# The last 3x3 convolution in tiles of four columns, with new pacing of the work beside the samplings

## Chip, cores, metric

The kernel runs on one core of a Trainium2 chip. The metric is the device time of one execution in microseconds; the profile of one execution is read along with it.

## What is computed

Four blocks act on `x` of 4 images x 256 channels x 64 x 64, each on a group norm of `x` and added back to it. The fourth adds its own input, too.

```python
x = x + _L0_conv_ref(_gn(x), ...)   # 1x1 conv, depthwise 3x3, deformable sampling, outproj, squeeze, two linear maps
x = x + _L1_conv_ref(_gn(x), ...)   # qkv 1x1, depthwise 5x5, linear attention, proj
x = x + _L2_conv_ref(_gn(x), ...)   # 3x3 convolution, 256 -> 256, weights scale*sign(w)
x = x + _L3_conv_ref(_gn(x), ...)   # attention against 2x2-pooled keys, 1x1 conv
```

In block 0 each pixel, group (4) and point (9) gathers four neighbours at computed places. Block 2 is an ordinary 3x3 convolution:

```python
scale = jax.lax.stop_gradient(jnp.mean(jnp.abs(real_w), axis=(1, 2, 3), keepdims=True))
bin_no_grad = scale * jnp.sign(real_w)
...
return jax.lax.conv_general_dilated(x, bin_w, window_strides=(STRIDE, STRIDE), padding=[(PAD, PAD), (PAD, PAD)], ...)
```

## The kernel before

All data is float32. Channels lie on the 128 partitions in two halves (`KT`), pixels on the free axis.

The images go through in a pipeline. For each image `sample` runs 288 rounds. A round issues four indirect DMAs on POOL (L596), which fetch table rows into one of seven buffers `g`, and eight small matmuls (L603) that weigh and sum them into `acc`, one bank in two halves. Two rounds fill a half; then ACT copies it (L608), PE turns it (L613), ACT copies again (L623). Every 18 rounds `project` (L636) applies the output projection. ACT makes the weights `wm` (L588).

`beside` (in `run`) interleaves other generators into these rounds. Each has a total of costs and a span `lo` to `hi` of the rounds' share. After each round a generator is advanced while what it has spent, by the numbers that it yields, is behind its due part of the total. What is left at `hi` is emitted at once. Beside the sampling of image n run:

- `feedforward` (end of block 0) of image n-1, from 0 to 0.22, total `FEED`
- `layer1` (block 1) of image n-1, from 0.22 to 1, total `LINEAR`
- `second`: `layer2` and then `layer3` (blocks 2 and 3) of image n-2, from 0.22 to 1, total `SECOND`; only beside the samplings of images 2 and 3
- `binarise`, the convolution's weights, beside the sampling of image 1, from 0 to 0.2

Inside `ordered()` PE, DVE, ACT and POOL run their instructions in the order in which they are emitted. An instruction that waits holds up everything behind it on its engine. Outside it the framework's scheduler sets the order.

`layer1` keeps a list `later` of closures, of which `step` pops one at each yield; a closure adds a `cost` of its own (L803). `summed` (L898) closes the sums of one half of the attention, `output` (L913) computes one band of its result, with `head` (L931) taking a bank for each `rden`. `groupnorm` (L112) needs two small matmuls with DVE work between.

After the last sampling come the last `feedforward` and `layer1` beside most of `second` for image 2, then the last `layer2` beside the rest of `second`, outside `ordered()`, and at the end the last `layer3`.

`layer2` convolves pairs of columns from four transformed inputs (two outputs from four products instead of six). It works on bands of 8 rows: `normed` loads and scales ten rows, `parts` (L1039) makes four sums and differences, 48 matmuls of 256 columns follow (L1088), and `leave` (L1068 to L1072) combines the products and adds the input.

```python
                        ps = self.long().rearrange("p (e q) -> p e q", e=2)
                        for i in range(12):
                            e, k, t = i // 6, i // 3 % 2, i % 3
                            nc.tensor.matmul(ps[:, e], w[:, k, t, 2 * half + e, m * P:(m + 1) * P], v[:, 2 * half + e, k, t:t + 8],
                                             start=i % 6 == 0, stop=i % 6 == 5)
```

`long` takes banks `acc` and `dp` in turn once the samplings are over. `layer3` computes scores (L1188), their maximum and exponential, turns them (L1200), multiplies by the values (L1206), scales (L1211), and after four such steps applies a 1x1 convolution (L1216) and adds the scaled input `r` (L1217, L1218).

Of the kernel before, what the change touches and what calls it, by code (L numbers as in the profile page):

```python
# [17 lines left out]
P = 128  # L18
# [18 lines left out]

CONVOLVE, OFFSETS, BINARY = NB * 9 + 26, 60, 62  # L40
FEED = NB * 40 + 8
LINEAR, LAST = 956, 624
STEPS, BEGUN = 900, 0.22
CONV, SECOND = NB * 22.5 + 11, 568
EPS_BN = 1e-5
EPS_GN = 1e-5
EPS_ATT = 1e-5
# [24 lines left out]
class Net:  # L72
# [36 lines left out]
        for k in range(KT):  # L109
            self.nc.vector.bn_stats(st[:, k, b, :], x[:, k])  # L110

    def groupnorm(self, pool, st, name):  # L112

        nc = self.nc
        mv = pool.tile([P, KT, 2], F32, name=name + "_mv")
        for k in range(KT):
            nc.vector.bn_aggr(mv[:, k, :], st[:, k].rearrange("p b s -> p (b s)"))
        yield 2
        pg = self.ps(name + "_pg")
        nc.tensor.matmul(pg[:, 0:KT], self.bd8, mv[:, :, 0], start=True, stop=True)  # L120
        mg = pool.tile([P, KT], F32, name=name + "_mg")
        nc.vector.tensor_copy(mg, pg[:, 0:KT])
        d = pool.tile([P, KT], F32, name=name + "_d")
        nc.vector.tensor_tensor(d, mv[:, :, 0], mg, ALU.subtract)
        nc.vector.tensor_tensor(d, d, d, ALU.mult)
        nc.vector.tensor_tensor(d, d, mv[:, :, 1], ALU.add)
        yield 2
        pv = self.ps(name + "_pv")
        nc.tensor.matmul(pv[:, 0:KT], self.bd8, d, start=True, stop=True)
        sc = self.rsqrt(pool, pv[:, 0:KT], EPS_GN, KT, name)  # L130
        bi = pool.tile([P, KT], F32, name=name + "_bi")
        nc.vector.scalar_tensor_tensor(bi, mg, -1.0, sc, ALU.mult, ALU.mult)
        yield 4
        return sc, bi

    def folded(self, pool, out, w, sc, bi, name):
# [67 lines left out]
    def setup(self):  # L204
# [45 lines left out]

        self.s_d = [dt([HW * PT, G * 5], F32, name=f"sd{n}") for n in im]
        self.w2_d = dt([P, KT, 3, 4, C], F32, name="w2")

    def binarise(self):


        nc = self.nc
        parts = [(k, slice(t, t + 3)) for k in range(KT) for t in range(0, 9, 3)]
        with self.tc.tile_pool(name="bin", bufs=1, side="left") as sp, \
                self.tc.tile_pool(name="bin2", bufs=2, side="left") as bp:  # L260

            def real(part):
                k, t = part
                w = bp.tile([P, 3, C], F32, name="w")
                nc.sync.dma_start(w, self.a["w2T"][:, k, t])
                return w

            sums = sp.tile([P, 6, C], F32, name="sums")
            for i, part in enumerate(parts):
                w = real(part)  # L270
                yield 1
                t = bp.tile([P, 3, C], F32, name="t")
                nc.vector.scalar_tensor_tensor(t, w, -1.0, w, ALU.mult, ALU.max)
                nc.vector.tensor_reduce(sums[:, i], t.rearrange("p t o -> p o t"), AX.X, ALU.add)
                yield 2
            ps = self.ps()
            for i in range(6):
                nc.tensor.matmul(ps[:, 0:C], self.ones, sums[:, i], start=i == 0, stop=i == 5)
            scale = sp.tile([P, C], F32, name="scale")
            nc.scalar.activation(scale, ps[:, 0:C], AF.Copy, scale=1.0 / (C * 9))  # L280
            yield 2
            for part in parts:
                w = real(part)
                yield 1
                t = bp.tile([P, 3, C], F32, name="t")
                s = bp.tile([P, 3, C], F32, name="s")
                nc.vector.tensor_scalar(t, w, 0.0, None, ALU.is_lt)
                nc.vector.scalar_tensor_tensor(s, w, 0.0, t, ALU.is_gt, ALU.subtract)
                nc.vector.tensor_tensor(s, s, scale.unsqueeze(1).to_broadcast([P, 3, C]), ALU.mult)
                yield 3  # L290
                nc.vector.tensor_scalar(t, w, -1.0, 1.0, ALU.max, ALU.min)
                nc.vector.tensor_tensor(s, s, t, ALU.subtract)
                nc.vector.tensor_tensor(s, s, t, ALU.add)
                yield 2
                u = bp.tile([P, 4, C], F32, name="u")
                nc.scalar.copy(u[:, 0], s[:, 0])
                nc.scalar.activation(u[:, 1], s[:, 2], AF.Copy, scale=-1.0)
                nc.scalar.activation(t[:, 0], s[:, 1], AF.Copy, scale=0.5)
                nc.vector.tensor_tensor(t[:, 1], s[:, 0], s[:, 2], ALU.add)
                for e, op in ((2, ALU.add), (3, ALU.subtract)):  # L300
                    nc.vector.scalar_tensor_tensor(u[:, e], t[:, 1], 0.5, t[:, 0], ALU.mult, op)
                nc.sync.dma_start(self.w2_d[:, part[0], part[1].start // 3], u)
                yield 2


# [451 lines left out]
    def layer1(self, n, st, st2):  # L757
# [3 lines left out]
        with tc.tile_pool(name=f"la{n}", bufs=1, side="right") as sp, \  # L761
# [35 lines left out]
            def staged(items):  # L797


                for i in range(len(items) + max(map(len, items)) - 1):  # L800
                    now = [it[i - k] for k, it in enumerate(items) if 0 <= i - k < len(it)]
                    later.append(lambda now=now: [f() for f in now])
                    later[-1].cost = 1.1  # L803

            sums = self.ps1.tile([P, 2, 2, P], F32, name="vk", tag="vk")
            ks = [sp.tile([P, 2, NB], F32, name=f"ks{t}") for t in range(2)]
# [91 lines left out]
            def summed(t):  # L898

                ln = bp.tile([P, 2, P], F32, name="ln", tag="v1")  # L900
                pc = self.ps("comb").rearrange("p (e o) -> p e o", e=2)
                for kind in range(2):
                    j = 2 * kind + t
                    nc.vector.tensor_tensor(ln[:, kind], sums[:, t, kind], self.con("bd"), ALU.mult)
# [1 line left out]
                    nc.vector.tensor_reduce(kk, ks[t][:, kind, 0:(NB, NCH)[kind]], AX.X, ALU.add)  # L906
                    for h in range(2):
                        nc.vector.tensor_scalar(ld[:, j, h, 16 * h:16 * h + 16], self.con("oh"), kk, None, ALU.mult)
                for kind in range(2):
                    nc.tensor.matmul(pc[:, kind], ln[:, kind], pw[:, 2 * kind + t], start=True, stop=True)  # L910
                    nc.vector.tensor_copy(pw[:, 2 * kind + t], pc[:, kind])

            def output(c, qp, aq):  # L913
# [17 lines left out]
                def head(h, j):  # L931
                    if not j:
                        xv.append(self.block(bp, self.x3_d[n], 2 * c + h, "xq", bufs=room(1)))
                    hs, i = slice(64 * (j // 2), 64 * (j // 2) + 64), 2 * h + j % 2
                    vk = alone and next(spare) == "vk"
                    pb[h, j] = self.ps1.tile([P, 512], F32, name="rden", tag="vk") if vk else self.ps("rden")
                    nc.tensor.matmul(pb[h, j], self.con("sel")[hs, i * P:(i + 1) * P], rd[0][hs], start=True, stop=True)  # L937

# [85 lines left out]
                    yield from aggregate(*args, **more)  # L1024
                    number += 1
            while later:
                yield step(2 if alone else 1)


    def layer2(self, n, st, st3, side="left"):  # L1030
# [3 lines left out]
        with tc.tile_pool(name=f"ca{n}", bufs=1, side=side) as sp, \  # L1034
                tc.tile_pool(name=f"cb{n}", bufs=2, side=side) as bp:
            w = sp.tile([P, KT, 3, 4, C], F32, name="w2")
            nc.sync.dma_start(w, self.w2_d)
            sc, bi = yield from self.groupnorm(sp, st, "g2")
            add = lambda out, a, b, op=ALU.add: (nc.gpsimd if self.alone else nc.vector).tensor_tensor(out, a, b, op)  # L1039

            def normed(b):
# [58 lines left out]
            before.pop()()  # L1100


    def layer3(self, n, st, wide=False):
        nc, tc, a = self.nc, self.tc, self.a
        M = HW // 4
        with tc.tile_pool(name=f"na{n}", bufs=1, side="left") as sp, \
# [6 lines left out]
            nc.sync.dma_start(gw, a["g_wT"])  # L1113
            ww = sp.tile([P, C], F32, name="ww")
            nc.sync.dma_start(ww, a["wz_wT"])
            sc, bi = yield from self.groupnorm(sp, st, "g3")

            sc1 = sp.tile([P, KT], F32, name="sc1")
            nc.vector.tensor_scalar(sc1, sc, 1.0, None, ALU.add)
# [1 line left out]
            nc.vector.tensor_tensor(bi1, bi, self.vec("wz_b", n=2), ALU.add)  # L1121

            bb = sp.tile([P, KT, P], F32, name="bb")
            ps = self.ps()
            for k in range(KT):
                nc.vector.tensor_scalar(bb[:, k], self.ones, bi[:, k:k + 1], None, ALU.mult)
                nc.tensor.matmul(ps[:, 0:P], bb[:, k], gw[:, k], start=k == 0, stop=k == KT - 1)
            gb = sp.tile([P, P], F32, name="gb")
            nc.vector.tensor_tensor(gb, ps[:, 0:P], self.row("g_b"), ALU.add)
# [46 lines left out]
            for b in range(NB):  # L1176
                m2 = bp.tile([P, 512], F32, name="m2")
                for j in range(4):
# [25 lines left out]
                    ps = self.ps()  # L1204
                    for m in range(8):
                        nc.tensor.matmul(ps[:, 0:P + 1], pT[:, m], gt[:, m], start=m == 0, stop=m == 7)  # L1206
                    yield 1.5
                    rden = bp.tile([P, 1], F32, name="rden")
                    nc.vector.reciprocal(rden, ps[:, P:P + 1])
                    yield 1.5  # L1210
                    nc.scalar.activation(m2[:, j * P:(j + 1) * P], ps[:, 0:P], AF.Copy, scale=rden)  # L1211
                yield 1.5
                r = self.block(bp, self.x5_d[n], b, "r5", bufs=1)
                for k in range(KT):
                    ps = self.ps()
                    nc.tensor.matmul(ps, ww[:, k * P:(k + 1) * P], m2, start=True, stop=True)  # L1216
                    nc.scalar.activation(r[:, k], r[:, k], AF.Identity, bias=bi1[:, k:k + 1], scale=sc1[:, k:k + 1])  # L1217
                    nc.vector.tensor_tensor(r[:, k], r[:, k], ps, ALU.add)  # L1218
                nc.sync.dma_start(self.out[n, :, b * 512:(b + 1) * 512].rearrange("(k p) s -> p k s", p=P), r)

    def run(self):
# [40 lines left out]
        with self.tc.tile_pool(name="gather", bufs=2, side="left") as self.gp, \  # L1262
# [16 lines left out]
            with ordered():  # L1279
                beside(self.sample(1, ssum[1]), rounds, (self.binarise(), BINARY, 0, 0.2), *behind(0))  # L1280
                for n in range(2, N):
                    beside(self.sample(n, ssum[n]), rounds, *behind(n - 1), (second(n - 2), SECOND, BEGUN, 1))
        self.idle, self.alone, self.spare = cycle(["acc", "dp"]), True, True
        rest = second(N - 2)
        with ordered():
            beside(range(STEPS), STEPS, (feed(N - 1), FEED, 0, 0.27), (linear(N - 1), LAST, 0.27, 1), (rest, SECOND, 0.27, 1.05))
        self.spare = False
        beside(range(STEPS), STEPS, (conv(N - 1, "right"), CONV, 0, 1), (rest, 150, 0, 1))

        self.banks = cycle(["mm", "mm", "mm", "vk"])  # L1290
        for _ in pooled(N - 1, True):
# [95 lines left out]
```

## Time and profile before

| | us |
|---|---|
| median of 3 runs (7638.07 to 7640.4) | 7640.25 |
| time of the profiled execution | 7631.35 |
| its span | 7629.6 |
| first gather, last gather (L596) | 138.8, 6117.3 |
| last `feedforward` (L714 to the last L749) | about 6180 to 6402 |
| last `layer1`, beside `second` of image 2 | about 6402 to 7232 |
| last `layer2` | about 7232 to 7418 |
| last `layer3` | about 7418 to 7630 |

Busy over the span: PE 5886.1 us (77%), POOL 4936.3 (65%), DVE 4810.4 (63%), ACT 3530.1 (46%). A row of the trace for PE is half of a float32 matmul of the program: the last convolution's 384 matmuls are 768 rows. The matmul rows overlap, so their mean duration is more than the distance from one to the next. A wait is put down to the instruction that ended last.

### The profile page before, as it was taken

To read this page: it belongs to the slowest core of one execution; us is meant where nothing else is said; L and a number is where in the kernel's file an instruction comes from. 1 tells how busy PE (TensorE), PEld (TensorE's weight loads), DVE (VectorE), ACT (ScalarE), POOL (GpSimd) and SP (SyncE) were. 2 spreads that over 40 slices of the span, in tenths; PEclk is the share of its full clock that TensorE was granted. 3 is DMA by queue.
4 is the path that set the end of the run, shared out by engine and by line. 5 is a ranking of instruction groups with operands and counts; after the bars stand their busy time and mean duration, and the time that the engine had idled before them with its cause. 6 is when DMAs were issued, how large, how long until landed. Compare 5 with 4: busy or idle time off the path is not lost. (4 is left out here: it accounts for less than half of the span.)

```text
span 7629.6 us, 99735 instructions
## 1 busy us (share of the span) xinstructions
PE 5886.1 (77%) x35776; PEld 3454.3 (45%) x35776; DVE 4810.4 (63%) x6045; ACT 3530.1 (46%) x10767; POOL 4936.3 (65%) x4870
## 2 busy tenths in 40 slices
PE   5676666678766677888877778988677789967899
PEld 2333333334433333346644443466444445744487
DVE  6454543633688776228988872279888734999623
ACT  2443433444545443445555544454555523655415
POOL 2777777777777777777777676777776702866210
PEclk7676776779877777999988889999888899988999
DMA  6564655565544444555544445455544432210221
GB/s 185 150 188 140 174 170 145 168 185 164 167 124 131 125 141 135 171 150 154 158 147 138 134 138 175 135 168 156 153 133 140 130 103 71 72 53 34 73 81 51
DMA packets 744383, 1031.75 MB, mean 135 GB/s; under 512 B 354128, under 2 KB 459984, under 8 KB 742352
## 3 DMA queue, kind: packets, MB, share of 16 engines
q0 software_dynamic: 221184, 604.27, 27.4%
q1 hardware_dynamic: 522704, 421.10, 18.6%
q8 instruction: 283, 4.64, 0.3%
q14 instruction: 212, 1.74, 0.1%
HBM read 856.39 MB, written 168.61 MB: 134 GB/s over the span
## 5 line engine op out<-in xcount | busy, mean ns | idle before, releaser
L596 POOL DMA_INDIRECT g<-tab,sl x4608 | 4401.1, 955 | 1715.8 <-issue 1271.0
L178 DVE SCALAR_TENSOR_TENSOR agg<-pad,vec,agg 128x1024 f32<-128x1024 f32 x2280 | 2933.7, 1287 | 64.4
L603 PE MATMUL acc<-g,wm 128*32 128x128 f32 x18432 | 1264.0, 321 | 1161.9 <-ACT at L608 670.8
L588 ACT ACTIVATE wm<-sl,con 128x48 f32<-128x48 f32 x6144 | 1487.8, 365 | 23.6 <-DMA sl<-sd 11.9
L603 PEld LDWEIGHTS acc<-g,wm 128*32 128x32 f32 x18432 | 622.1, 121 | 1836.7 <-ACT at L608 888.3
L1088 PE MATMUL ps<-xd,w 128*128 128x256 f32 x3072 | 721.6, 386 | 8.0 <-DVE x L1072 3.5
L1088 PEld LDWEIGHTS ps<-xd,w 128*128 128x128 f32 x3072 | 579.9, 194 | 116.6 <-issue 35.6
L623 ACT COPY dT<-dp 64x128 f32<-64x128 f32 x1152 | 295.5, 256 | 646.4 <-PE dp L613 379.7
L739 PE MATMUL ps<-x2f,f 128*128 128x512 f32 x1024 | 489.8, 625 | 4.0 <-ACT f L714 4.0
L724 DVE SCALAR_TENSOR_TENSOR hm<-ps,vec,lk 128x512 f32<-128x512 f32 x256 | 191.9, 750 | 466.7 <-ACT lk L741 466.2
L824 PE MATMUL ps<-xr,qw 128*128 128x512 f32 x768 | 461.1, 732 | 13.8 <-ACT pT L1202 5.2
L749 PE MATMUL ps<-hm,f 128*128 128x512 f32 x1024 | 468.0, 604 | 0.0
L1039 POOL TENSOR_TENSOR xd<-xp 128x640 f32<-128x640 f32 x64 | 79.6, 1270 | 514.2 <-ACT xp L1051 416.1
L608 ACT COPY at<-acc 128x256 f32<-128x256 f32 x576 | 214.1, 372 | 423.1 <-PE acc L603 411.2
L741 ACT ACTIVATE lk<-ps,low 128x512 f32<-128x512 f32 x256 | 175.9, 687 | 500.5 <-PE ps L739 498.2
L1206 PEld LDWEIGHTS ps<-gt,pT 128*128 128x128 f32 x2048 | 282.6, 216 | 85.9 <-ACT pT L1202 43.4
L1206 PE MATMUL ps<-gt,pT 128*128 128x129 f32 x2048 | 297.6, 304 | 29.8 <-ACT pT L1202 29.1
L613 PE MATMUL dp<-ident,at 128*128 128x128 f32 x1152 | 265.2, 317 | 65.7 <-ACT dT L623 62.9
L636 PE MATMUL po<-dT,ow 128*128 128x288 f32 x1024 | 297.3, 438 | 21.8 <-ACT dT L631 8.9
L1188 PE MATMUL s<-ph,th 128*128 128x512 f32 x512 | 281.6, 663 | 32.9 <-DVE ot L941 11.0
L200 POOL TENSOR_TENSOR ak<-ak,m 128x1024 f32<-128x1024 f32 x96 | 227.6, 2371 | 117.2 <-ACT m L196 112.8
L727 DVE TENSOR_TENSOR xyf<-xyf,ps 128x512 f32<-128x512 f32 x64 | 44.0, 687 | 402.1 <-PE ps L749 389.3
(243 smaller groups left out, 7565.2 us busy)
## 6 DMA issues: line engine op xcount, KB each, us to landing
g<-tab,sl POOLq DMA_INDIRECT x4608
x<-x SPq DMA_DIRECT2D x128, 512.0 KB
xr<-x SPq DMA_DIRECT2D x96, 512.0 KB
tab<-xo SPq DMA_DIRECT2D x192, 128.0 KB
x<-in_x SPq DMA_DIRECT2D x32, 512.0 KB
y<-yc SPq DMA_DIRECT2D x32, 512.0 KB
yb<-y SPq DMA_DIRECT2D x64, 256.0 KB
x<-yb SPq DMA_DIRECT2D x64, 256.0 KB
```

The costliest lines, as they stand in the source:

```text
L178: nc.vector.scalar_tensor_tensor(to, s, wt, acc, ALU.mult, ALU.add)
L588: nc.scalar.activation(wm[:, :, :, o], blocks[b][:, r:r + WR, G:], AF.Copy, scale=self.con("own")[:, o:o + 1])
L596: nc.gpsimd.indirect_dma_start(out=g[:, i, :], out_offset=None, in_=table, in_offset=bass.IndirectOffsetOnAxis(ap=sl.bitcast(I32)[:, r, i: ...
L603: nc.tensor.matmul(acc[32 * i:32 * i + 32, :], wm[:, r4, 4 * i + 2 * x:4 * i + 2 * x + 2, :], g[:, i, x * P:(x + 1) * P], start=x == 0, st ...
L623: nc.scalar.copy(dT[b][hs, :, r:r + UR], dp[u][hs, :, :, s, :].rearrange("p v g o -> p g v o"))
L636: nc.tensor.matmul(po[m][:, 0:BR * OB], self.ow[:, k, m * P:(m + 1) * P], dT[b][:, k].rearrange("p r o -> p (r o)"), start=k == 0, stop=k ...
L739: nc.tensor.matmul(ps, f1[:, k, m * P:(m + 1) * P], x2[:, k], start=k == 0, stop=k == KT - 1)
L749: nc.tensor.matmul(ps, f2[:, k, m * P:(m + 1) * P], hm[:, k], start=k == 0, stop=k == 4 * KT - 1)
L824: nc.tensor.matmul(ps, qw[:, k, m * P:(m + 1) * P], x[:, k], start=k == 0, stop=k == KT - 1)
L1088: nc.tensor.matmul(ps[:, e], w[:, k, t, 2 * half + e, m * P:(m + 1) * P], v[:, 2 * half + e, k, t:t + 8], start=i % 6 == 0, stop=i % 6 == 5)
L1188: nc.tensor.matmul(s[i], tv[:, 4 * b + j], ph[:, i * 512:(i + 1) * 512], start=True, stop=True)
L1206: nc.tensor.matmul(ps[:, 0:P + 1], pT[:, m], gt[:, m], start=m == 0, stop=m == 7)
```

## The change

1. The last `layer2` is replaced by `layer2_fours`: four columns from six transformed inputs (six products for four outputs), bands of 16 rows, three sets of weights `w[e]`, three banks. The additions of the transform are on DVE for the first band and on POOL for the others.
2. `binarise` also makes the weights for it (`w4`).
3. Beside the samplings: `groupnorm` gets pauses (`lag`), `bb` in `layer3` is made before a pause, `summed` leaves its matmuls to `combined`, two places later in `later`; `rden` takes every second bank from "vk"; in `layer3` the load of `r` and its scaling move between the steps of the block; closures cost 1.5 instead of 1.1.
4. Totals and starts follow: `BINARY`, `LINEAR`, `SECOND`, `CONV`, and the start of `second` at 0.25.

```diff
-CONVOLVE, OFFSETS, BINARY = NB * 9 + 26, 60, 62
+CONVOLVE, OFFSETS, BINARY = NB * 9 + 26, 60, 92
-LINEAR, LAST = 956, 624
+LINEAR, LAST = 990, 624
-CONV, SECOND = NB * 22.5 + 11, 568
+CONV, SECOND = 150, 617
...
-    def groupnorm(self, pool, st, name):
+    def groupnorm(self, pool, st, name, lag=0):
...
-        yield 2
+        yield 2 + lag
...
-        yield 4
+        yield 4 + lag
...
+                u = bp.tile([P, 6, C], F32, name="u4")
+                q = bp.tile([P, 2, C], F32, name="q")
...
+                nc.sync.dma_start(self.w4_d[:, part[0], part[1].start // 3], u)
+                yield 2
...
-                    later[-1].cost = 1.1
+                    later[-1].cost = 1.5
...
             def summed(t):
                 ln = bp.tile([P, 2, P], F32, name="ln", tag="v1")
-                pc = self.ps("comb").rearrange("p (e o) -> p e o", e=2)
+                later[0:0] = [lambda: None, partial(combined, t, ln)]
...
+            def combined(t, ln):
+                pc = self.ps("comb").rearrange("p (e o) -> p e o", e=2)
                 for kind in range(2):
                     nc.tensor.matmul(pc[:, kind], ln[:, kind], pw[:, 2 * kind + t], start=True, stop=True)
+                for kind in range(2):
                     nc.vector.tensor_copy(pw[:, 2 * kind + t], pc[:, kind])
...
-                    vk = alone and next(spare) == "vk"
+                    vk = next(spare) == "vk"
...
             while later:
-                yield step(2 if alone else 1)
+                yield step(2 if alone else 1.6)
...
-            sc, bi = yield from self.groupnorm(sp, st, "g2")
+            sc, bi = yield from self.groupnorm(sp, st, "g2", 3)
...
+    def layer2_fours(self, n, st, st3):
+        R, V = 16, W // 4
...
+            w = [sp.tile([P, KT, 3, 2, C], F32, name=f"w{e}") for e in range(3)]
+            for e in range(3):
+                for k in range(KT):
+                    nc.sync.dma_start(w[e][:, k], self.w4_d[:, k, :, 2 * e:2 * e + 2])
...
+                stt(pq[:, 0], col(2), -4.0, col(4), ALU.mult, ALU.add)
+                stt(pq[:, 1], col(1), -4.0, col(3), ALU.mult, ALU.add)
+                add(a[:, 0], pq[:, 0], pq[:, 1], ALU.add)
+                add(a[:, 1], pq[:, 0], pq[:, 1], ALU.subtract)
+                yield a
+                r, u, a = new("pr", bufs=1), new("pu", bufs=1), new("vb")
+                add(flat(r), two(4), two(2), ALU.subtract)
+                add(flat(u), two(2), two(0), ALU.subtract)
+                yield
+                stt(a[:, 0], u[:, 1], 2.0, r[:, 0], ALU.mult, ALU.add)
+                stt(a[:, 1], u[:, 1], -2.0, r[:, 0], ALU.mult, ALU.add)
+                yield a
+                a = new("vc")
+                stt(a, u, -4.0, r, ALU.mult, ALU.add)
+                yield a
...
+            for c in range(NCH):
...
+                for m in range(KT):
+                    for e in range(3):
+                        ps = self.long().rearrange("p (e q) -> p e q", e=2)
+                        for i in range(12):
+                            j, k, t = i // 6, i // 3 % 2, i % 3
+                            nc.tensor.matmul(ps[:, j], w[e][:, k, t, j, m * P:(m + 1) * P], now[e][:, j, k, t:t + R],
+                                             start=i % 6 == 0, stop=i % 6 == 5)
...
-            sc, bi = yield from self.groupnorm(sp, st, "g3")
+            sc, bi = yield from self.groupnorm(sp, st, "g3", 0 if wide else 3)
...
+            for k in range(KT):
+                nc.vector.tensor_scalar(bb[:, k], self.ones, bi[:, k:k + 1], None, ALU.mult)
+            yield 3
...
+                    if j == 1:
+                        r = self.block(bp, self.x5_d[n], b, "r5", bufs=1)
+                    if j == 3:
+                        for k in range(KT):
+                            nc.scalar.activation(r[:, k], r[:, k], AF.Identity, bias=bi1[:, k:k + 1], scale=sc1[:, k:k + 1])
                     yield 1.5
...
-                yield 1.5
-                r = self.block(bp, self.x5_d[n], b, "r5", bufs=1)
                 for k in range(KT):
+                    yield 1.5
                     ps = self.ps()
                     nc.tensor.matmul(ps, ww[:, k * P:(k + 1) * P], m2, start=True, stop=True)
-                    nc.scalar.activation(r[:, k], r[:, k], AF.Identity, bias=bi1[:, k:k + 1], scale=sc1[:, k:k + 1])
                     nc.vector.tensor_tensor(r[:, k], r[:, k], ps, ALU.add)
+                yield 2
...
-                    beside(self.sample(n, ssum[n]), rounds, *behind(n - 1), (second(n - 2), SECOND, BEGUN, 1))
+                    beside(self.sample(n, ssum[n]), rounds, *behind(n - 1), (second(n - 2), SECOND, BEGUN + 0.03, 1))
...
-        beside(range(STEPS), STEPS, (conv(N - 1, "right"), CONV, 0, 1), (rest, 150, 0, 1))
+        self.idle = cycle(["acc", "dp", "vk"])
+        fours = self.layer2_fours(N - 1, st[2][1], st[3][1])
+        beside(range(STEPS), STEPS, (fours, CONV, 0, 1), (rest, 150, 0, 1))
```

## The prediction

> **What bounds the kernel now.** I first read the table of stretches over the span, because the engines' mean shares mix stages with different limits. Columns: window, length, then busy us and count of PE, PEld, DVE, ACT and POOL, granted clock, DMA share, GB/s.
>
> ```profile
> 1632.00:3120.00 1488.00, 1107.74 (x6828) 552.88 (x6829) 974.21 (x1019) 701.45 (x2437) 1124.66 (x1180) 0.79 0.50 147
> 3120.00:4620.00 1500.00, 1215.61 (x8310) 744.53 (x8308) 1052.91 (x1269) 762.96 (x2480) 1076.94 (x1131) 0.90 0.50 146
> 4620.00:6120.00 1500.00, 1202.39 (x8268) 735.31 (x8266) 1045.92 (x1256) 778.50 (x2545) 1071.54 (x1124) 0.90 0.51 149
> ...
> 6402.00:7232.00 830.00, 665.77 (x2728) 448.26 (x2728) 708.73 (x879) 452.26 (x642) 494.70 (x224) 0.89 0.20 62
> 7232.00:7418.00 186.00, 181.70 (x852) 158.00 (x852) 51.74 (x110) 25.37 (x35) 39.77 (x32) 0.99 0.27 81
> 7418.00:7630.00 212.00, 193.66 (x1040) 145.98 (x1040) 80.47 (x188) 107.33 (x200) 0.00 (x0) 0.97 0.16 55
> ```
>
> The last convolution (7232 to 7418) is PE from end to end, 181.7 of 186 us. So is most of the last attention. In the samplings no engine is full. There I counted gathers (L596) per 100 us, and who held POOL up in a window of the second sampling and in one of the fourth.
>
> ```profile
> 3400.00:3500.00 100.00, 65.26 (x69) 0.88 0.58 166
> ...
> 3600.00:3700.00 100.00, 75.93 (x80) 0.95 0.59 167
> ...
> 4600.00:4700.00 100.00, 55.75 (x60) 0.88 0.65 207
> ...
>   PE acc L603: 8.1, 15
> ...
>   issue: 303.1, 995
>   PE acc L603: 103.4, 59
> ```
>
> An undisturbed POOL gathers 80 times in 100 us, 5.0 us for a round of four. Beside one image's work (second sampling) it waited 8.1 us for PE, beside two images' work 88.0 and 103.4 us (third, fourth). From the starts of the gathers the 1152 of each image took 1465, 1452, 1513 and 1545 us, against 1152 x 1.25 = 1440.
>
> PE may trail by the seven buffers of g. Its lag, the start of a round's L603 less that of its last gather (both in the timeline), is at most 8 us through most of the second sampling's rounds 96 to 288. In the third it is 22 at round 0, 35 at 48, 40 at 72, 17 at 84, 32 at 144 and 32 at 276; never near zero. So in the third and fourth samplings the PE queue is the bound, and POOL stops where the lag reaches about 32. What PE itself waits for there (waits of PE, 3806 to 4180):
>
> ```profile
> PE acc L603 <- ACT at L608: 53.6, 29, 6.0
> ...
> PE g_pg L120 <- DVE g_mv L117: 6.5, 1, 6.5
> PE comb L910 <- DVE ln L904: 5.9, 1, 5.9
> PE ps L1160 <- DVE xq L1153: 5.4, 1, 5.4
> PE ps L1127 <- DVE bb L1126: 5.1, 1, 5.1
> ```
>
> The largest is the copy of acc, on an ACT queue that stands behind other copies. The lower four are single waits for DVE results asked for too soon.
>
> **What the Trainium skill says.** "TensorE: Matmul & The Clock Gate", Step-by-step, has matmuls stay in program order, with only weight loads pulled ahead. The trace agrees: L603 stands idle behind the waits above although its gathers landed long ago. "PSUM — Partial Sum Buffer", on bank collisions, asks for guards by bank, not by address. The trace agrees: L603 starts at 4575.66, just after L608's copy of the other half of the bank (4575.23, 0.37 us). "GPSIMD Engine Reference", Performance pitfalls, prices reads with steps over 8 bytes at 2.9 cycles an element instead of 1.9. The new transform reads every fourth float (16 bytes). No row here has that step on POOL; L1039 reads every second one, 1273 ns for 640 elements.
>
> **The change, part by part.** The sum is against the profiled 7631.35 us (span 7629.6), 8.9 below the shown median of 7640.25; I add the 8.9 at the end.
>
> Last convolution.
>
> ```profile
> L1088 PE MATMUL ps<-xd,w 128*128 128x256 f32 x768 | 168.9, 382 | 0.0
> ...
> L1039 POOL TENSOR_TENSOR xd<-xp 128x640 f32<-128x640 f32 x31 | 38.5, 1273 | 104.5 <-PE ps L1088 77.9 <-DVE m L1150 20.2 <-ACT xp L1051 6.4
> ```
>
> Before: 8 bands x 2 x 2 x 12 = 384 matmuls of 256 columns, two rows each, 768. After: 4 bands x 2 x 3 x 12 = 288, 576 rows. The chain of waits has 618 rows in 133.40 us, 0.216 each; 192 fewer save 41.4 us.
>
> What it adds lies beside PE. A band takes PE 144 x 0.216 = 31 us. On DVE I estimate four 576-element and one 1152-element transform op (4 x 0.75 + 1.4, from 820 ns for 640 on DVE), and six leaves of about 2.2 us (L1070 689 ns, L1071 422 ns, L110 693 ns): 18 us. On POOL two contiguous adds of 576 (1.15 each) and two of 1152: 2.3 each at L1039's rate, 3.5 at the page's price, so 7 to 9.3. ACT about 6. If a cover fails, a part late by x costs x once per band. The products stay 24 groups of 12 with three banks instead of two. SP's queue gets weights of 4.7 MB instead of 3.1 ahead of the first rows: at the 380 to 400 GB/s of the present load about 4 us later. The first transform is on DVE, two products and two sums (2.8 us) behind two activations of 1.2, where it was 1.75 us after 1.8.
>
> The start is set by the order of PE. Now about one and a half attention steps of image 2 stand between g_pv (7224.3) and the first product (7238.2). In the changed program it is three. Steps are 9.4 us apart (L1188 at 7208.8, 7218.3, 7227.6): 1.5 x 9.4 = 14 us later, hiding weights and transform, less 1.5 x 4.8 = 7 us of PE work that no longer lies among the products. Cost 7, bounds 0 and 15. Stage: -34.
>
> Samplings. Per round I summed PE's work in order of program, with 0.43 us for a 512-column row, 0.216 for 256, 0.165 for a transpose and 0.65 for L603. The total of an image is 1147 us in both programs; it moves. Us a round in blocks of 12 rounds from round 60: before 4.0, 3.9, 4.5, 4.3, 4.4, 4.2; after 3.1, 2.9, 4.5, 4.8, 4.7, 4.8. Rounds 216 to 288 fall from 4.2 to 4.07 in the mean.
> - Rounds 60 to 84: the second stage starts at 0.25 instead of 0.22, so its norm no longer meets linear's. These cost POOL 15 and 13 us over 5.0 a round; I take 4: -11. The lag at 84 is then again about 18.
> - Rounds 84 to 144: SECOND / (1 - start) goes from 728 to 823 against a list that grew only by pauses, so the products stand 13% closer. Added PE work is 20 us; the lag reaches 32 early and POOL pays 25 where it paid 5: +20.
> - Rounds 144 to 216: g_pg, bb, xq and comb waits (22.9 us together) mostly go by the lags of the norms, the split bb and the later comb. POOL lost 14; I take 2: -12.
> - Rounds 216 to 288: 10 us less PE work, and rden's use of the vk bank spares a wait of 5.5 for ot and some of 3.2 for r. POOL lost 30; I take 16: -14.
> - The border of third and fourth: about 29 us lost around 4627; a shorter tail of linear: -5, once. Its wm (7.3 us) and sd (8.4) waits stay.
> Per image -17, so -34 and -5: -39. Bounds -110 (lag gone, both at 1440 plus the border) and +40.
>
> The rest. The fours' weights in binarise add five DVE and four ACT instructions in each of six parts, and 4.7 MB of stores, beside a second sampling in which POOL waits 8 us; its DVE has about 500 us spare: 0, bounds 0 and +5. Stage 6402 to 7232 is DVE's (709 of 830); spacing PE there brings 0, bounds -6 and +6. In the last attention r's load and scaling move off the end of a block, PE is 193.7 of 212: -1.
>
> Sum -34 - 39 - 1 = -74: 7557 profiled, 7566 on the scale of the median.
>
> **Rivals.**
> 1. The samplings give nothing: what the waits free is eaten by the closer products. For it: PE's work is equal, lag never zero. Against: 23 us of named waits an image vanish. Time 7640 - 35 = 7605; 0.20.
> 2. The lag does vanish: waits on ACT shrink along with the others. For it: the second sampling shows 5.0 a round with the same linear work. Against: 342 us of L603's waits are behind ACT, which the change scarcely touches. 7640 - 35 - 105 = 7500; 0.12.
> 3. The convolution is not PE's: 16-byte steps on DVE and POOL, or banks held by slow leaves, keep PE waiting. It would need over 1.7 times the estimated DVE time. Convolution gain 0 to 15, samplings as forecast: 7595; 0.08.
> 4. Slower: in rounds 84 to 144 of the third and fourth samplings PE, at 4.7 us of 5.0, meets one more late ACT copy each round. Present waits there are about 1 us a round; at 2 us, 60 x 1 x 2 = 120 us, less the 74: 7686. It overtakes the gains from about 0.6 us a round. For it: with a lag at the limit nothing absorbs a wait. Against: the first stage at 4.7 runs at 5.0 to 5.5. 0.11.
>
> **The numbers.** The forecast case has 0.49, its own range 7540 to 7595. The cases give 7566 as the likeliest. The range 7498 to 7628 takes in rivals 1 and 3 and most of 2. About 0.2% (15 us) is what a measurement can tell. Faster: 0.49 + 0.20 + 0.12 + 0.08, less 0.05 for a rival 1 that also loses some 30 us = 0.84; same: those 0.05 and 0.01 of rival 4; slower 0.10.
>
> **What would show it.** The product line has 576 rows and its stage is 145 to 155 us with PE over 90% busy; the first product comes 10 to 20 us after the second norm's g_pv than before. POOL's wait for L603 falls from 88 and 103 to about 70 and 80, gathers are 80 per 100 us near 3450, and short of 80 near 3650. The waits of comb, bb and g_pg are under 2 us each. I am wrong if POOL's waits grow, if DVE's leaves release the products, or if the last stages lose what the convolution saves.

## The result, and the profile after

The changed kernel takes 7648.09 us (median of 12 runs, 7637.78 to 7651.28), the kernel before 7640.03 beside it (12 runs); the ratio is 1.001, 95% interval 1.0001 to 1.0018. The forecast was 7566. The profiled execution has a span of 7649.4 us against 7629.6, at the same granted clock of 0.84. The profiled execution of the changed kernel is the slowest of its 12 and that of the kernel before lies 8.9 us below its median, so that the spans differ by 19.8 us where the medians differ by 8.1.

From the starts of the gathers and the first and last row of each stage (us):

| | before | after | difference |
|---|---|---|---|
| first, second sampling | 1464.7, 1453.8 | 1464.4, 1457.1 | 0, +3 |
| third, fourth sampling | 1513.8, 1546.2 | 1547.1, 1577.0 | +33, +31 |
| last gather | 6117.2 | 6184.5 | +67.3 |
| last gather to the first row of the last `feedforward` | 78.4 | 74.7 | -4 |
| `feedforward` | 205.6 | 205.6 | 0 |
| from there to the end of the last `layer1` | 810.9 | 802.9 | -8 |
| from there to the first product | 26.1 | 36.5 | +10 |
| products of the last convolution | 178.4 | 132.4 | -46 |
| last product to the end | 212.9 | 212.9 | 0 |

What stands behind the last gather fell by 47.5 us, what stands ahead of it grew by 67.3.

The groups of the page of the changed kernel, busy us and mean ns of one, then idle us before them and its main releaser. They answer to L596 and L603 of before:

```profile
L611 POOL DMA_INDIRECT g<-tab,sl x4608 | 4404.1, 956 | 1779.9 <-issue 1271.3
...
L618 PE MATMUL acc<-g,wm 128*32 128x128 f32 x18432 | 1270.9, 322 | 1227.0 <-ACT at L623 735.5
```

The gathers last as long as before; POOL stands idle 64 us more (1715.8 before), and PE's accumulating rows stand behind ScalarE's copy of `acc` 65 us more (670.8 before). The same in the third sampling alone, PE's waits before and after: us in total, times, longest.

```profile
PE acc L603 <- ACT at L608: 168.9, 87, 12.5
PE dp L613 <- ACT dT L623: 17.7, 8, 3.3
```

```profile
PE acc L618 <- ACT at L623: 202.3, 94, 11.5
PE dp L628 <- ACT dT L638: 19.9, 10, 3.3
```

And POOL's wait for PE in the same stretch, before and after:

```profile
POOL g L596 <- PE acc L603: 81.3, 53, 7.6
```

```profile
POOL g L611 <- PE acc L618: 115.7, 57, 7.9
```

POOL waits 34.4 us more for PE, and the sampling is 33 us longer; in the fourth it is 41.4 (110.1 to 151.5) and 31. PE's wait for the copy grew by 33.4 us, and by 32.5 in the fourth (175.2 to 207.7). That this is the same size doesn't make it the cause: 14.7 of the 33.4 lie in rounds 60 to 84 (9.1 to 23.8), in which the sampling became shorter. The stretches of the third sampling before and after (length, then busy us and count of PE, PEld, DVE, ACT, POOL, granted clock, DMA share, GB/s) show that PE's idle time as a whole grew by 12.0 us only, because its other waits fell, and its busy time by 21.0 (as the profile has it, with the ends of the rows modelled):

```profile
3057.00:4571.00 1514.00, 1218.05 (x8309) 744.52 (x8308) 1049.23 (x1263) 782.09 (x2554) 1097.16 (x1152) 0.90 0.51 149
```

```profile
3060.00:4607.00 1547.00, 1239.02 (x8337) 757.30 (x8336) 1051.29 (x1266) 782.33 (x2557) 1097.68 (x1152) 0.89 0.49 146
```

In the fourth, idle time grew by 15.8 us and busy time by 15.2.

How a copy comes late is seen in a piece of the changed kernel's timeline: start, duration, engine, line, and in brackets the idle time before it.

```profile
4207.26 0.64 PE L618 MATMUL acc<-g,wm 128*32 128x128 f32 x16
...
4207.83 1.98 PE L839 MATMUL ps<-xr,qw 128*128 128x512 f32 x4
...
4209.85 0.78 ACT L851 ACTIVATE pad<-ps,g_add,vec 128x512 f32<-128x512 f32 x1 [3.61 <-PE ps L839]
...
4211.50 1.06 ACT L876 ACTIVATE av<-av 128x1024 f32<-128x1024 f32 x1 [0.54 <-DVE av L178]
...
4212.46 1.25 ACT L1328 ACTIVATE pe<-s,mx 128x512 f32<-128x512 f32 x2
...
4213.19 0.66 PE L1334 MATMUL pt<-ident,pe 128*128 128x128 f32 x4 [3.37 <-ACT pe L1328]
4213.60 0.52 ACT L638 COPY dT<-dp 64x128 f32<-64x128 f32 x2
...
4214.13 0.37 ACT L623 COPY at<-acc 128x256 f32<-128x256 f32 x1
...
4214.56 1.08 PE L618 MATMUL acc<-g,wm 128*32 128x128 f32 x16 [0.72 <-ACT at L623]
```

A half of `acc` is done at 4207.90, but its copy starts at 4214.13: ScalarE's queue has `linear`'s L851 and L876 and the second stage's exponentials ahead of it, and these wait for PE and VectorE. Only after the copy does PE begin the other half, which lies in the same bank. The copy is the end of a chain here: PE first stood idle 3.37 us for the exponentials (L1328) and then 0.72 us for the copy.

The last convolution did what it should. Groups of the changed kernel from 7290 to 7445:

```profile
L1216 PE MATMUL ps<-va,w 128*128 128x256 f32 x192 | 43.9, 384 | 1.2 <-DVE va L1161 1.2
L1216 PE MATMUL ps<-vc,w 128*128 128x256 f32 x192 | 42.9, 379 | 0.0
L1216 PE MATMUL ps<-vb,w 128*128 128x256 f32 x192 | 42.7, 379 | 0.0
...
L1166 POOL TENSOR_TENSOR pu<-xp 128x1152 f32<-128x1152 f32 x3 | 10.6, 3517 | 0.0
...
L1160 DVE SCALAR_TENSOR_TENSOR pq<-xp 128x576 f32<-128x576 f32 x4 | 9.2, 2291 | 0.0
```

576 rows with 1.2 us of idle time. The two products of the transform (L1159, L1160) and its adds on POOL are slow, but they run beside PE.

### The profile page after: what moved, and what is told of

It reads as the page before. It is cut to its first block, busy times and chain, and to the rows that moved or that the text cites. A ratio compares the mean times of both kernels' runs of the same rounds, so it can differ in the third digit from the quotient of the medians.

```text
span 7649.4 us, 99404 instructions
## 1 busy us (share of the span) xinstructions
PE 5873.6 (77%) x35584; PEld 3434.8 (45%) x35584; DVE 4878.2 (64%) x6099; ACT 3538.8 (46%) x10807; POOL 4929.3 (64%) x4850
## 5 line engine op out<-in xcount | busy, mean ns | idle before, releaser
L603 ACT ACTIVATE wm<-sl,con 128x48 f32<-128x48 f32 x6144 | 1486.3, 365 | 23.4 <-DMA sl<-sd 11.8
L1107 PE MATMUL ps<-xd,w 128*128 128x256 f32 x2304 | 545.5, 387 | 0.0
L1107 PEld LDWEIGHTS ps<-xd,w 128*128 128x128 f32 x2304 | 436.4, 195 | 83.8 <-issue 29.8
L651 PE MATMUL po<-dT,ow 128*128 128x288 f32 x1024 | 312.9, 455 | 26.9 <-DVE yb L658 16.4
L754 PEld LDWEIGHTS ps<-x2f,f 128*128 128x128 f32 x1024 | 192.1, 196 | 230.2 <-issue 220.3
L893 ACT COPY kt<-pt 128x512 f32<-128x512 f32 x256 | 148.6, 582 | 316.6 <-PE pt L889 315.9
L764 PEld LDWEIGHTS ps<-hm,f 128*128 128x128 f32 x1024 | 189.5, 191 | 225.5 <-issue 225.3
```

The source lines that it names most:

```text
L603: nc.scalar.activation(wm[:, :, :, o], blocks[b][:, r:r + WR, G:], AF.Copy, scale=self.con("own")[:, o:o + 1])
L651: nc.tensor.matmul(po[m][:, 0:BR * OB], self.ow[:, k, m * P:(m + 1) * P], dT[b][:, k].rearrange("p r o -> p (r o)"), start=k == 0, stop=k ...
L754: nc.tensor.matmul(ps, f1[:, k, m * P:(m + 1) * P], x2[:, k], start=k == 0, stop=k == KT - 1)
L764: nc.tensor.matmul(ps, f2[:, k, m * P:(m + 1) * P], hm[:, k], start=k == 0, stop=k == 4 * KT - 1)
```

## The experiments

Four parts of the pacing were first taken apart. "Last gather" and "rest" (the span after it) are from each run's trace; those of the kernel before are 6117.2 and 1512.4, of the changed one 6184.5 and 1464.9. Kernels that are to do the same ahead of the last gather differ there by 4 us (the kernel before and e1) to 9 us (e8b and e10b), so parts of less than 10 us aren't resolved.

**e1_tail_only: the new convolution, everything beside the samplings old.**

```diff
 before.py
+layer2_fours, its weights w4, BINARY 92, CONV 150, banks acc, dp, vk at the end
```

> The kernel before with the four-column convolution and its weights alone; all pacing beside the samplings as before. In the changed kernel the last gather came at 6184.5 us (before: 6117.2) and what follows it took 1465 us (before: 1512). If the pacing alone costs the samplings their time (theory A), the last gather stays at 6115 to 6122 and the total falls by about 45 us, to 7590 to 7600. If the fours' weights in binarise or their stores disturb the samplings (rival B), the last gather comes 10 us or more later than 6117, and the total falls by less than 35.

7599.93 us (5 runs; before 7637.79), ratio 0.995, interval 0.9936 to 0.9964. Last gather 6113.6, rest 1484.6. The convolution gains; the new pacing loses 70.9 us up to the last gather, and with it the rest is 20 us shorter.

**e2_linear_old: the changed kernel with `linear`'s pacing of before.**

```diff
-LINEAR = 990; later[-1].cost = 1.5; yield step(2 if alone else 1.6)
+LINEAR = 956; later[-1].cost = 1.1; yield step(2 if alone else 1)
```

> The changed kernel with linear's old pacing: closures at 1.1, total 956, last steps at 1. Theory A1 (the second stage, started later and emptied faster, overfills PE's rounds): last gather stays within 15 us of 6184. Theory A2 (linear's new pacing puts its closures where PE is full): last gather falls to 6150 or below.

7629.9 (one run). Last gather 6153.8: 30.7 us of the loss are back, not all; it lies between the two theories.

**e3_rden_old: `rden` takes "vk" only after the samplings.**

```diff
-vk = next(spare) == "vk"
+vk = alone and next(spare) == "vk"
```

> The changed kernel with rden in the common banks beside the samplings, as before. A1 and A2: within 10 us of 6184, or later. Theory A3 (rden's own bank lets PE run ahead of DVE and ACT and puts matmuls ahead of L618 in its queue): 20 us or more earlier.

7652.04 (one run), last gather 6186.6. No effect that could be resolved.

**e4_start_old: `second` starts at 0.22 again.**

```diff
-(second(n - 2), SECOND, BEGUN + 0.03, 1)
+(second(n - 2), SECOND, BEGUN, 1)
```

> The changed kernel with the second stage started at 0.22 again, its total of 617 kept: it is emptied at 2.75 a round instead of 2.86 (before: 2.53). A1 with the late start as its cause: last gather at 6150 or below. A1 with the longer list or the pauses as its cause, or A2: within 15 us of 6184.

7643.47 (one run), last gather 6169.2: 15.3 us back, which is at the edge of "within 15". With e2's 30.7 this left some 25 unexplained, to which the next two runs were put: the edits of e2 and e4 together, and the three numbers of `linear`'s new pacing (those of e2's diff, reversed) on top of e1. The expectation of e6b also speaks of a place in the list; that edit isn't in the kernel that ran, it is in the fourth column of the table below.

> The changed kernel with linear's old pacing (1.1, 956, step 1) and the old start of the second stage; its pauses, its read of r and the denominators' vk stay as changed. The last gather ended at 6113.6 us with everything beside the samplings old, at 6184.5 with everything new; undoing linear's pacing alone gave 30.7 back, undoing the start alone 15.3. If the two costs add: last gather 6138 (6133 to 6143), some 25 us left for the second stage's own list, time about 7612. If the two are one stall seen from two sides (late copies): last gather 6153 or later. If only their meeting costs and the second stage's list is free: 6110 to 6122, time about 7590.

> The new last convolution with nothing new beside the samplings but linear's pacing (1.5, 990, step 1.6, the projection's denominators put ahead in the list). If linear's pacing costs by itself: last gather 6113.6 + 31 = 6144 (6139 to 6149), time about 7627 (the later stage's linear part gives 5 to 8 us back). If it costs only where the second stage is late too: 6110 to 6122, time about 7595.

e5b: 7594.69 (2 runs; before 7638.69), ratio 0.9942 (0.9922 to 0.9962), last gather 6109.1. e6b: 7610.23 (4 runs), ratio 0.9963 (0.9948 to 0.9978), last gather 6135.2. Neither theory of a plain sum held:

| `linear`'s three numbers | start of `second` | pauses, read of `r`, `combined`, `rden` | last gather (us) | against e1 |
|---|---|---|---|---|
| old | 0.22 | old | 6113.6 | 0 |
| old | 0.22 | new | 6109.1 | -4.5 |
| new | 0.22 | old | 6135.2 | +21.6 |
| old | 0.25 | new | 6153.8 | +40.2 |
| new | 0.22 | new | 6169.2 | +55.6 |
| new | 0.25 | new | 6184.5 | +70.9 |

The fourth column alone costs nothing. With it in, the later start costs 44.7 us beside the old `linear` and 15.3 beside the new; `linear`'s numbers cost 60.1 with the old start, 30.7 with the new, and 21.6 where the fourth column is old. Parts that can't be added point to a shared limit that each runs into.

**e8b_two_banks: that limit.** The suspect was the bank. This is e1 again, with the halves that the samplings write in turn in different banks; the two banks and their sizes are the same, and no instruction's shape changes. Each bank is one tile of the program, so the halves also come to lie in different tiles; which of the two the wait goes by isn't told apart.

```diff
-accs, dps = halves("acc"), halves("dp")
+t = [self.ps1.tile([P, 2, 256], F32, name=name, tag=name) for name in ("acc", "dp")]
+accs, dps = cycle([t[0][:, 0], t[1][:, 0]]), cycle([t[1][:, 1], t[0][:, 1]])
```

> The new last convolution, old samplings, and the two halves that the samplings write in turn lie in different PSUM banks. Theory one, PE waits for ScalarE's copy of the other half of its bank before it may start a half (670.8 us over the whole run) and this sets the pace of the third and fourth sampling: their lengths fall from 1515 and 1543 to 1450 to 1490 us, time 7470 to 7530. Theory two, the gathers or PE's own work set the pace and the wait only takes up slack: 1505 to 1545 us each, time 7590 to 7605.

7449.25 us (4 runs; before 7638.69), ratio 0.9747, interval 0.9731 to 0.9763. Third and fourth sampling 1448.5 and 1470.9 us, last gather 5973.8. The time is below theory one's range, and theory two is out. PE's waits in the third sampling:

```profile
PE ps L1330 <- ACT pT L1326: 24.2, 18, 4.7
PE dp L624 <- ACT at L619: 23.4, 5, 12.9
```

The accumulating rows' wait for ScalarE is gone from the list; what is left of the copy is the transpose that reads its result. POOL waits 5.2 and 2.1 us for the rows of `dp` and `acc` instead of 81.3. The stretch of the third sampling of this kernel, to be set against that of the kernel before, shown above (e1, from which this one is edited, takes 1516 us there with 1219.12 busy):

```profile
3054.00:4503.00 1449.00, 1198.26 (x8317) 729.12 (x8316) 1047.92 (x1264) 777.98 (x2555) 1096.48 (x1153) 0.91 0.53 156
```

PE has the same 8300 rows in 65 us less. Of these, 45 are idle time of PE (295.95 to 250.74) and 20 are shorter busy time for as many rows. So PE's rows alone did not set the pace of the third and fourth samplings; the waits in its queue did their part. The third is now about as long as the second (1453 us), which PE hardly holds up; the fourth, at 1470.9, stays some 18 us above that.

**e9_after_banks: the changed kernel, with the two banks.**

> The changed kernel whole, with the halves in different banks. Theory one, the new pacing costs because it puts more work of ScalarE and VectorE ahead of the copies that PE waits for bank by bank: without that wait the 71 us between the two pacings shrink to under 25, the last gather comes at most 25 us after that of the two-bank kernel with the old pacing, time within 10 us of it. Theory two, the new pacing costs because it heaps PE's own work in rounds that had room for less: the 60 to 70 us stay, time 45 to 55 us above that kernel.

7474.46 us (4 runs; before 7638.69), ratio 0.9788, interval 0.9772 to 0.9805; last gather 6009.2, rest 1460.8. The new pacing costs 35.4 us at the last gather instead of 70.9: between the theories. With the two banks half of its cost is gone. What PE waits for in its third sampling:

```profile
PE acc L624 <- ACT at L619: 37.3, 8, 11.3
PE ps L1336 <- ACT pT L1332: 32.3, 19, 7.2
PE pt L1330 <- ACT pe L1324: 28.5, 17, 4.2
```

The first line is now a wait for data: L624 are the transposes that read the copy. In both banks they wait 51.5 us for it, 26.5 in e8b. The second and third are PE's waits for the second stage's exponentials and their copies. But PE's idle time as a whole is hardly longer than in e8b, 254.4 us against 250.7; its busy time is 16.3 longer:

```profile
3049.00:4518.00 1469.00, 1214.58 (x8334) 739.56 (x8323) 1049.23 (x1266) 776.75 (x2557) 1098.37 (x1153) 0.90 0.53 153
```

From round 84 on the busy time is even 34.3 us longer than in e8b (812.61 to 846.90) and the idle time 14.3 us shorter, so that 20 us are paid. In one bank all of the 43 us of added busy time were paid (see "Why the prediction was wrong"). So e9 fits two readings that it doesn't tell apart: fewer late copies, or a PE with room for the work that the new pacing heaps there.

**e11b_banks_linear_old and e10b_all_best: the other half, and the best of both.** e11b is e9 with e2's edit. e10b is e8b with the new pacing only after the last gather:

```diff
-sc, bi = yield from self.groupnorm(sp, st, "g2")
+sc, bi = yield from self.groupnorm(sp, st, "g2", 3 * self.alone)
...
-later[-1].cost = 1.1
+later[-1].cost = 1.5 if alone else 1.1
```

and likewise for the other pauses, the read of `r` and `bb`.

> As e11, for a chip on which the kernel before takes about 7640 us. If what is left of the cost is linear's heaping of TensorE work in rounds 120 to 180: last gather 5975 to 5985. If it is the later start of the second stage: 5995 to 6010, with rounds 132 and 168 at 5.0 to 5.1 us and 228 to 264 at 5.2 to 5.4.

> As e10, for a chip on which the kernel before takes about 7640 us. If the two gains stand beside each other: last gather 5974 (5966 to 5982), the rest after it 1461 to 1470 us, time 7430 to 7446. If the rest is short only because linear's work was pushed into the samplings: the rest stays at 1475 or more, time 7448 or more.

e11b: 7456.19 (2 runs; before 7646.69), ratio 0.9756 (0.9736 to 0.9775), last gather 5985.5, rounds 228 to 264 at 5.01 to 5.07 us. With two banks the later start of `second` is within what isn't resolved (2 to 12 us above e10b and e8b), and most of what remained went with `linear`'s pacing. e10b: 7449.79 (4 runs), ratio 0.9748 (0.9732 to 0.9765), last gather 5983.1, rest 1464.9. The rest does keep its gain with nothing new beside the samplings (1477.1 in e8b), but the last gather came 9 us later than in e8b, so the time is e8b's. These two are the fastest kernels of this study.

**A second set of runs.** e5, e6, e7, e8, e10 and e11 ran where the kernel before takes 8743 and 8733 us. The expectations of e10b and e11b speak of a chip, but the record gives chip 1 for e5 to e8 as for e1 to e4, where it takes 7638, and chip 7 for e10 and e11; what makes the difference isn't known. The programs of e5, e6, e8, e10 and e11 are those of the runs with a b. Their times: e7 (e1 with the second stage's pauses only after the samplings) 8713.77, ratio 0.9966 (0.9955 to 0.9977); e8 8630.57, 0.9873 (0.9849 to 0.9897); e10 8601.07, 0.9848 (0.9831 to 0.9864); e11 8595.18, 0.9845 (0.9829 to 0.9862); e5 and e6 8717.25 and 8713.88 (one run each). The kernels with two banks lead there too, with half to three fifths of the gain. Their lengths can't be set against the other runs'.

> The kernel before with the four-column convolution, and with the second stage's pauses, its bb and its r moved only in what follows the samplings. Last gather 6113 to 6120, since nothing beside the samplings differs. In the changed kernel the stretch from the last feedforward to the end of the last linear took 803 us, in the kernel with the convolution alone 819. If the pauses are the cause: 800 to 808 here, total 7585 to 7592. If not (rden's bank or the split sums is the cause, or chance of the lists): 815 or more, total near 7600.

e7's stage from `feedforward` to the end of `layer1` took 808.8 us, against 805.5 in e5 and 814.0 in e6 beside it: within what isn't resolved.

## Why the prediction was wrong

The forecast was 82 us too low, and a gain was forecast where there is none. One term did it, the samplings: forecast -39, measured +67 in the profiles. Two steps of it failed:

- "Per round I summed PE's work". For rounds 216 to 288 this gave 10 us less work; PE was busy 19.8 us longer there, and 18.1 in the fourth. For rounds 144 to 216 the forecast has no term for work, although by its own figures the total stays the same while rounds 60 to 84 lose 23 us, 84 to 144 gain 20 and 216 to 288 lose 9, which leaves some 12 us more for 144 to 216.
- "Mostly go": waits that end were credited to POOL nearly in full, as if nothing else on PE's queue would take their place. PE's idle time from round 84 on did not fall at all.

By blocks of rounds (third and fourth sampling, from the gathers; PE's busy and idle time in the third, between the same gathers, in differences to the kernel before):

| rounds | forecast | measured | PE busy | PE idle |
|---|---|---|---|---|
| 60 to 84 | -11 | -9.2, -7.0 | -19.9 | +10.9 |
| 84 to 144 | +20 | +13.0, +16.1 | +16.9 | -3.9 |
| 144 to 216 | -12 | +8.1, +9.6 | +6.2 | +1.8 |
| 216 to 288 | -14 | +21.9, +21.3 | +19.8 | +2.2 |
| border, once | -5 | -9.4 (rounds 0 to 60 of the fourth) | | |

From round 84 to the end the third sampling took 43 us more. PE's busy time grew by 42.9 there (834.95 to 877.83, with 6233 rows instead of 6111), its idle time by 0.1; in the fourth it is 47, 45.0 and 2.0. About 20 us of this are work that no longer lies in rounds 60 to 84, where PE had 100 rows fewer. The rest is rows that took longer and smaller shifts, which were not followed further; the granted clock of rounds 216 to 288 was 0.85 instead of 0.87.

- The first two blocks and the border went as forecast, and by the shifts that the prediction counted.
- Rounds 144 to 216. The waits named in the prediction mostly went: comb 5.9 to 1.9, bb and xq from 5.1 and 5.4 to none; g_pg grew from 6.5 to 8.8. PE's waits from 3813 to 4195 of the changed kernel answer to the lines shown there:

```profile
PE acc L618 <- ACT at L623: 67.0, 30, 11.5
PE g_pg L120 <- DVE g_mv L117: 8.8, 1, 8.8
...
PE comb L928 <- ACT m L1350: 1.9, 1, 1.9
```

  The wait for `acc` rose from 53.6 to 67.0. Together the five are 76.5 us before and 77.7 after. The prediction had the guard in hand (L603 right after the other half's copy) and listed the 53.6 as the largest wait, and then credited the small ones nearly in full.
- Rounds 216 to 288. Here it is PE's busy time, by the stretches before and after:

```profile
4180.00:4572.00 392.00, 303.77 (x2061) 171.71 (x2060) 310.32 (x347) 201.42 (x647) 274.23 (x289) 0.87 0.47 138
```

```profile
4195.00:4609.00 414.00, 323.56 (x2096) 185.51 (x2096) 293.79 (x333) 203.06 (x653) 273.96 (x289) 0.85 0.44 131
```

  The waits changed places: that for `acc` rose from 47.2 to 55.8, that for the exponentials (`pt`) from 4.1 to 11.5, and `den` waits 4.7 for `av`; the waits for `ot` and part of those for `r` went, 7.5 us, as forecast. The prediction's price for the `den` products, 0.43 us for each 512-column row, is also too high by itself, since they run four at once (below).
- Rival 1, "what the waits free is eaten", had the right objection and too small a price. Rival 4 came nearest, with a loss through PE's queue while the lag is at its limit. Its mechanism, one more late copy each round in rounds 84 to 144, isn't in the trace: the wait for the copy fell there from 35.7 to 30.7 us, and the block lost no more than forecast. Rounds 144 to 288 lost 30 us each image, where a gain was forecast. "Against" rival 2 it was said that the change scarcely touches the waits behind ACT. That for the copy became longer by 33 us an image.

What stood right: the convolution's term was -34, measured -46 for the products and +10 for the start, -36. That the sum came out so close is in part luck, since both sizes were off and their errors cancel. 576 rows were right; the difference from -41.4 to -46 is of the size of the attention steps that no longer lie among the products, which the prediction had booked at the start (7 us). The first product comes 24.5 us after g_pv instead of 13.9, 10.6 later (forecast 10 to 20). Of the four 576-element operations of the transform on DVE, the two that read every fourth float from both sources took 2.2 and 2.3 us, not 0.75, the others 0.76 and 1.06; the 1152-element adds on POOL 3.5 and 2.8 against an estimate of 2.3 to 3.5. DVE is busy 96.8 of the 133 us, so it stayed hidden and rival 3 didn't come. The stage of the last `layer1` gave 8 us where 0 (-6 to +6) was put. It is there in e5b too (805.0), where `linear`'s numbers are old, and not in e1 (818.9); which of the other edits makes it wasn't tried. But e1 and the kernel before have the same program in this stage and differ by 8.0 us themselves, so a gain of 8 isn't resolved. POOL's waits, forecast to fall, grew, which the prediction had named as the sign that it is wrong; near 3450 POOL made 75 gathers in 100 us, not 80.

What stays open: which place in ScalarE's order makes the copies late was read from the timeline and not tried by moving the copy. That the waits on the bank shared by both halves hold back the third and fourth samplings is shown by e8b, where 45 of 65 us are idle time of PE. That the new pacing loses its time through these waits is not shown: its loss stands in PE's busy time, and e9 shows only that half of it goes when PE has room. Why the other half goes with `linear`'s pacing (e11b), and why PE's rows take longer, was not followed further.

## What to carry to other kernels

When an engine trails its producer by a constant lag, ask whether it is late by work or by waits: give the wait's resource a second copy and see whether the same rows take less time, before any work is moved. Before a wait that grew is taken for the cause, add up the busy and the idle time of the engine over the same rounds: here the one wait grew by 33 us and all idle time by 12. Halves that two engines use in turn are better laid in different banks, which cost nothing here, as there were two such pairs to be crossed; "PSUM — Partial Sum Buffer" of the Trainium skill, under its bank collisions, asks for the guard by bank, and here it cost 151 us of 7600 (e1 to e8b). Small waits that ended earlier brought nothing here: of the 22.9 us that were named, 10.7 were left, and PE's idle time in those rounds went from 109.9 to 111.6 us.

## What was not expected of the hardware

- The eight `den` products of 512 columns, on 32-column tiles, go four at a time. In the changed kernel's timeline their 16 rows run from 4215.41 to 4218.30, 2.9 us, and rows of four tiles start within 0.02 us of each other; at the prediction's 0.43 us for each row it would be 6.9.
- The same rows show what a lower clock costs. From 4214.1 to 4217.4 the granted clock was 0.50, and the `den` rows that started at 4215.41 and 4216.26 took 1.06 to 1.07 us; those that started at 4217.71, after it, took 0.59. Just before, PE had stood idle for 3.37 us. That the lower clock came from the idle time is not shown by a run.
- The same program (e8 and e8b) had a span of 8619.9 us once and 7450.8 the other time, at clocks of 0.80 and 0.85. A gather took 954 and 956 ns, but POOL stood idle before gathers for 2749.8 against 1569.5 us, 770.3 of them, in 347 waits, until an event whose source the trace doesn't tell ("remote").
- A copy of 0.37 us, 142 of them in a sampling, held up PE for 202 us in the changed kernel: the wait is its place in the queue, not its length.
